# Two queries of a token side by side, and a place of their own for relu and its sum, in a fused time-mix and expert kernel

## The chip, the core and the metric

The kernel runs on one core of a Trainium2 chip. The metric is the device time of one execution in microseconds (us). The core's engines run side by side, each with its own instruction list in a fixed order: TensorE (PE; its weight loads are listed as PEld), VectorE (DVE), ScalarE (ACT), GpSimd (POOL) and SyncE (SP), which issues DMAs. They meet only through semaphores. A matrix product reads two operands from the on-chip memory SBUF: the stationary one, which is loaded into the array as weights first, and the moving one, which is streamed past it. It writes to the accumulator memory PSUM.

## What is computed

The input x has 2 sequences of 2048 tokens with 256 channels, all in float32. After a layer norm two branches are computed and multiplied:

```python
xn = layernorm(x)
s  = timemix(xn)            # RWKV-7 style recurrence, 4 heads of 64 channels
g  = silu(ffn(xn))          # two experts per token, LoRA on a shared 256->1024->256 net
out = x + s * g

# the recurrence of timemix, for each head; S is 64 x 64
sa = S @ a_t                # a_t = -k
S  = S * d_t + outer(sa, b_t) + outer(v_t, kk_t)
y  = S @ r_t

# the experts
inter = xn @ wi.T + bi + (xn @ lora_A[e].T) @ lora_B[e].T
out  += gate_e * (relu(inter) @ wo.T + bo)
```

So each token has two queries, a and r (both are multiplied onto the state), and two keys, b and kk.

## The kernel before

The tokens are handled in 16 blocks of 256 (128 of each sequence). Each block is cut into chunks of 64 tokens (L = 64), so it has 2 chunks (k) for each of 2 sequences (b). Heads come in pairs: `pair` and `par` (which half of the 128 partitions) name a head. Within a chunk the recurrence is turned into matrix products. For this the decays of the state are spread over six levels with h = 1, 2, 4, 8, 16, 32: at level h the chunk is cut in runs of h tokens, and for each pair of neighbouring runs the queries of the second run meet the keys of the first.

The stages of a block are generators: `norm`, `front` (gates of the experts), `mixes` (projections that give r, a, b, kk, v), `levels`, `chunks` (carries the state over, gives y, group norm, output) and `experts`. Each of them yields numbers, the times at which its next step is due, counted in turns; a block begins every 12 turns. A heap runs the steps of all blocks in the order of these numbers. The instructions of every engine are issued in that order and stay in it. The numbers are in the table `AT`, in which a name such as "rank", "op" or "query4" is the place of a step; `PROFILE`, `PROFILE0`, "first" and "last" spread the experts' steps over the turns. Steps with the same number run in the order of the stages, older blocks first.

The steps and buffers that matter here:

- `AR` (L424) holds a block's queries: 128 partitions x 2 queries x 516, all of a and then all of r; r is shifted by one token. `BK` (L426) holds the keys in the same way. ACT writes r into AR from PSUM (L438) and a (L515); POOL reads r for `rk` (L519).
- `products` (L548) multiplies, at each level, the keys of a chunk (stationary) with the queries of the second runs (moving, 64 columns) for all heads, in 64 x 64 corners of the array. Each float32 product is two PE instructions, so there are 64 for each level. They go to two PSUM tiles `lev`, one for each `par`.
- `take_products` (L554) copies what the level's mask allows of `lev` into the pair matrices `D`: two masked copies (COPY_PREDICATED) per level, each of 512 elements per partition. `D` (L240) has 16 rows of DW = 66 words for each `par`: a row for each (chunk, pair, key, query).
- `decay_on` multiplies the queries of the second runs by the decay so far (DVE, L580) and the keys of the first runs (POOL, L583).
- `first_inverse`, `inverse1`, `transposed` and `inverse2` (L607, L623, L617, L630) build the inverse of a triangular matrix in `X` by levels, with `take_inverse` (L634), a masked copy into X, just before `take_products` of the next level.
- `chunks` uses slices of D as weights (L790, L847: `pair_matrix`), and of AR (L809).
- `last_queries` (L563, L566) and `lastr` (L688) handle the last r of a chunk.
- `experts` goes through eight parts f of the hidden layer: `basep` (PE, L938), `base` (ACT, L940), `lop` (PE, L943), `hs` = lop + base for both experts (DVE, L945), relu in place (ACT, L946), and the sum over the two experts into `hT` (POOL, L947). `fop` (L957) multiplies hT by the second weight. `hs` has two buffers.
- `psf` gives PSUM tiles from a pool of four, in turn. Nearly all stages, `lev`, `basep`, `lop`, `miu` and `op` among them, take theirs from it, so that a product can start only when the tile taken four requests before has been read.

Of the kernel before, what the change touches and what calls it, by code (L numbers as in the profile page):

```python
# [34 lines left out]
def timemix_gated_by_lora_experts(ctx: ExitStack, tc: tile.TileContext, a: dict, out: bass.AP):  # L35
# [50 lines left out]
    def load_x(i):  # L86
# [10 lines left out]
        "stats": 5.82, "root_x": 9.97, "inv_x": 10.32, "xn": 10.79, "xTp": 11.66, "dx": 11.66, "xm": 11.84,  # L97
        "lgp": -0.16, "mixp": 0.44, "top": 0.52, "gt": 2.1, "rank": 3, "ex": 3.27, "vsum": 3.94, "mix12": 2.29,
# [4 lines left out]
        "gmean": 6.13, "ysq": 7.26, "gvar": 7.91, "root_y": 9.38, "inv_y": 10.72, "scale": 10.84, "gp": 11.69,  # L103
        "ygp": 12.23, "op": 14.55, "la": -1.34, "first": 0.46, "last": 0.94, "ex0": 0.8, "ex15": 0.9, "ex16": 0.6,
        "ready": 5.51, "const": 4.33, "rv": -0.8, "sa0": 0.2, "up0": 1.2, "uv0": 2.2, "sa1": 3.2, "up1": 4.2,
        "uv1": 5.2,
    }
    PROFILE = [0.88, 1.2, 0.8, 1.66, 0.32, 1.18, 0.01, 0.5, 1.72, 1.5, 1.03, 1.98]
    PROFILE0 = [0.61, 0.53, 1.28, 1.83, 0.05, 0.7, 0.45, 0.41, 1.6, 1.55, 0.66, 3.1]
# [61 lines left out]
    mask = const.tile([P, len(LEVELS), LMAX], U8, name="mask")  # L171
    maskT = const.tile([P, len(LEVELS), LMAX], U8, name="maskT")

    def mask_parts():
        for m, second in ((mask, 0), (maskT, 1)):
            mf = hold.tile([L, len(LEVELS) * LMAX], F32, name=f"mf{second}")
            nc.gpsimd.memset(mf, 1.0)
            for li, h in enumerate(LEVELS):
                n, lo = LMAX // h, second * h
                mv = mf[:, li * LMAX : (li + 1) * LMAX].rearrange("p (n h) -> p n h", h=h)  # L180
                nc.gpsimd.affine_select(out=mv, in_=mv, compare_op=ALU.is_ge, fill=0.0, base=-lo,
                                        pattern=[[-2 * h, n], [0, h]], channel_multiplier=1)
                nc.gpsimd.affine_select(out=mv, in_=mv, compare_op=ALU.is_ge, fill=0.0, base=lo + h - 1,
                                        pattern=[[2 * h, n], [0, h]], channel_multiplier=-1)
                yield
            nc.gpsimd.tensor_copy(m[half(0)], mf.rearrange("p (l c) -> p l c", c=LMAX))

            nc.sync.dma_start(out=m[half(1)], in_=m[half(0)])
# [27 lines left out]


    def order(h):
        return "n h"

    def mask_of(m, li, h, k):
        v = m[:, li, :].rearrange(f"p (n h) -> p {order(h)}", h=h)
        return v.unsqueeze(1).broadcast_to([P, k, *v.shape[1:]])

    def runs(ap, h, which):

        if len(ap.shape) == 2:
            return ap.rearrange("p (n w h) -> p n w h", w=2, h=h)[:, :, which, :].rearrange(f"p n h -> p {order(h)}")
        return ap.rearrange("p m (n w h) -> p m n w h", w=2, h=h)[:, :, :, which, :].rearrange(f"p m n h -> p m {order(h)}")
# [10 lines left out]
    Dbuf = [hold.tile([P, 2, 8 * NK, DW], F32, name=f"D{j}") for j in range(2)]  # L240
# [147 lines left out]
    def mixes(i):  # L388
# [35 lines left out]
        AR = q["AR"] = sb2.tile([P, 2, 516], F32, tag="AR", name=f"AR{i}")  # L424

        BK = q["BK"] = sb2.tile([P, 2, 2 * SUP], F32, tag="BK", name=f"BK{i}")  # L426
        rv = AR[:, 1, 1:513].rearrange("p (c t) -> p c t", c=2)
        av = AR[:, 0, 0:512].rearrange("p (c t) -> p c t", c=2)
# [96 lines left out]
    def levels(i):  # L525
# [17 lines left out]
        def products(li, h):  # L543
            levp = [psf(f"lev{i}_{h}_{par}").rearrange(f"p (m q {order(h)}) -> p m q {order(h)}", m=4 * NK, q=2, h=h)
                    for par in range(2)]
            for key in range(2):
                for k, pair, b, par, rows, c0 in blocks():
                    matmul(levp[par][half(b), (k * 2 + pair) * 2 + key], BK[rows, key, c0 : c0 + L],  # L548
                           runs(AR[rows, :, c0 : c0 + L], h, 1), start=True, stop=True)
            return levp  # L550

        def take_products(li, h, levp):
            for par in range(2):
                nc.vector.copy_predicated(  # L554
                    runs(D[:, par, :, 0:L], h, 1), mask_of(mask, li, h, 8 * NK),
                    levp[par].rearrange("p m q x y -> p (m q) x y"))

        def last_queries():

            lp = [psf(f"last{i}_{par}")[:, 0 : 4 * NK].unsqueeze(2) for par in range(2)]  # L560
            for key in range(2):
                for k, pair, b, par, rows, c0 in blocks():
                    matmul(lp[par][half(b), (k * 2 + pair) * 2 + key, :], BK[rows, key, c0 : c0 + L],  # L563
                           AR[rows, 1, c0 + L : c0 + L + 1], start=True, stop=True)
            for par in range(2):
                nc.vector.tensor_copy(  # L566
                    D[:, par].rearrange("p (m q) v -> p m q v", q=2)[:, :, 1, L : L + 1], lp[par])

        def decay_on(h):

            np_ = SUP // h
            bpv = q["bp"].rearrange("p (n w) -> p n w", w=2)

            def decay(which):
                v = bpv[:, :, which : which + 1].broadcast_to([P, np_, h]).rearrange(f"p n h -> p {order(h)}")
                return v.unsqueeze(1).broadcast_to([P, 2, *v.shape[1:]])

            yield TURNS * i + AT[f"query{h}"]
            qa = runs(AR[:, :, 0 : 2 * SUP], h, 1)
            nc.vector.tensor_tensor(qa, qa, decay(0), ALU.mult)  # L580
            yield TURNS * i + AT[f"key{h}"]
            ka = runs(BK, h, 0)
            nc.gpsimd.tensor_mul(ka, ka, decay(1))  # L583
# [15 lines left out]
        def by_run(t, h):  # L599
            return t.rearrange(f"p m ({order(h)}) -> p m {order(h)}", h=h)  # L600

        def first_inverse():

            nt = ps_inv.tile([P, 2, 512], F32, tag="inv", name=f"n{i}")[:, :, 0 : NK * 2 * LMAX]
            nt = nt.rearrange("p z (m n) -> p z m n", n=LMAX)
            for k, pair, b, par, rows, c0 in blocks():
                matmul(nt[half(b), par, k * 2 + pair, :], AR[rows, 0, c0 : c0 + L],  # L607
                       runs(BK[rows, 0, c0 : c0 + L], 1, 0).squeeze(2), start=True, stop=True)
            for par in range(2):
                xv = X.rearrange("p (m z) (n w) -> p z m n w", z=2, w=2)[:, par, :, :, 0]  # L610
                nc.vector.copy_predicated(xv, maskT[:, 0, :].unsqueeze(1).broadcast_to([P, NK * 2, LMAX]),
                                          nt[:, par])
# [6 lines left out]
        def inverse1(li, h, m1):  # L619

            m1 = by_run(m1, h)
            for e, k, b, m in each():
                matmul(m1[half(b ^ k), m], D[half(b), e % 2, (k * 2 + e // 2) * 4, 0:L],  # L623
                       runs(X[half(b), m, :], h, 0), start=True, stop=True)
# [40 lines left out]
        for li, h in list(enumerate(LEVELS))[1:]:  # L665
# [17 lines left out]
            else:  # L683
                last_queries()
                lastr = AR[:, 1, 1:513].rearrange("p (m t) -> p m t", t=L)[:, :, L - 1 : L]
# [4 lines left out]
    def chunks(i):  # L690
# [14 lines left out]
        def pair_matrix(k, b, par, pair, key, query):  # L705
            return D[half(b), par, ((k * 2 + pair) * 2 + key) * 2 + query, query : query + L]
# [89 lines left out]
        for k in range(NK):  # L796
# [116 lines left out]
    def experts(i):  # L913
# [18 lines left out]
        hT = sb1.tile([P, DFF // P, SUP], F32, tag="hT", name=f"hT{i}")  # L932
        for f in range(DFF // P):
# [9 lines left out]
            matmul(lop, lBT[:, 0, fc], lat, start=True, stop=True)  # L943
            hs = sb2.tile([P, 2, SUP], F32, tag="hs", name=f"hs{i}_{f}")
            nc.vector.tensor_tensor(hs, lop, bs.unsqueeze(1).broadcast_to([P, 2, SUP]), ALU.add)  # L945
            nc.scalar.activation(hs, hs, AF.Relu)  # L946
            nc.gpsimd.tensor_add(hT[:, f, :], hs[:, 0, :], hs[:, 1, :])  # L947
# [49 lines left out]

    parts = [constants()]
# [4 lines left out]
    while queue:  # L1003
        at, n = queue[0]
        after = next(parts[n], None)
# [41 lines left out]
```

## Time and profile before

| | before |
|---|---|
| runs | 1121.29, 1124.88, 1119.23 us |
| median | 1121.29 us |
| profiled execution, its own time | 1120.85 us |
| its span in the profile | 1119.1 us |
| granted TensorE clock, mean | 0.978 |
| masked copies into D, L554 | 192 instructions, 181.4 us of DVE |
| relu, L946 | 128 instructions, 80.6 us of ACT, 142.5 us idle before them |
| sum over experts, L947 | 128 instructions, 93.5 us of POOL, 205.5 us idle before them |
| loads of D's slices in `inverse1`, L623 | 2560 loads, 46.0 us of PEld |

In the page the busy line gives for each engine its busy time, the share of the span and the number of instructions. The chain follows the work that ended last back from the end, and gives the share of each engine in it. A line of the waits reads "who waited, on whom: us in total, times, longest". A line of the timeline reads "start, duration, engine, line, operation, output<-inputs, sizes and number of instructions merged", and in brackets the idle time of the engine before it and who ended it. In the page's groups, a duration behind a comma is the mean of one instruction in ns. Durations of neighbouring instructions of an engine may overlap a little.

### The profile page before, as it was taken

The numbers are of one execution on the slowest core, as the hardware profiler recorded it, in microseconds if no ns is written. First come the engines' busy times: TensorE is split into PE (matmuls) and PEld (weight loads), VectorE is DVE, ScalarE is ACT, GpSimd is POOL, SyncE is SP. The second block draws the span as 40 slices with busy tenths as digits, with TensorE's granted clock in tenths as the row PEclk, the third lists the DMA queues.
The fourth block names the chain that finished last, engine by engine and source line by source line (L and its number), as shares of the span: only waits on it lengthen the run. The fifth ranks groups of instructions, "written<-read, shape, count | busy, mean of one in ns | idle before, by whom it ended". The sixth has DMA issues, their size and how long they took to land.

```text
span 1119.1 us, 51172 instructions
## 1 busy us (share of the span) xinstructions
PE 1056.6 (94%) x23136; PEld 823.2 (74%) x23136; DVE 720.6 (64%) x1613; ACT 573.0 (51%) x1372; POOL 659.6 (59%) x852
## 2 busy tenths in 40 slices
PE   6999999999999998999999999999999999999997
PEld 3677777777777776786777877777777777777865
DVE  5365866666585664757667576766767666685645
ACT  2625546372644636555463645546464553736363
POOL 6373657567474855747466573756757474674541
PEclk8989999999999998999999999999999999999999
DMA  8000000000000000000000000000000000000000
GB/s 230 19 3 2 3 3 4 22 3 22 2 22 3 3 22 3 21 4 3 21 3 22 3 22 3 3 22 4 22 3 13 4 3 13 3 12 3 14 3 20
DMA packets 16073, 17.02 MB, mean 15 GB/s; under 512 B 3248, under 2 KB 15472, under 8 KB 15856
## 3 DMA queue, kind: packets, MB, share of 16 engines
q1 hardware_dynamic: 15696, 13.62, 4.5%
q8 instruction: 182, 2.98, 1.1%
q14 instruction: 35, 0.29, 0.1%
q10 hardware_dynamic: 160, 0.13, 0.0%
HBM read 9.53 MB, written 4.19 MB: 12 GB/s over the span
## 4 chain that ended last, share of the span: by engine, by line
PE 72%; DVE 12%; POOL 4%; issue 3%; ACT 3%; DVEq 0%; POOLq 0%; ACTq 0%
PE fop L957 10%; PE basep L938 8%; PE lev L548 8%; PE lop L943 7%; DVE D L554 5%; PE m1p L623 4%; PE miu L402 3%; PE m1p L617 3%; PE rp L419 3%; PE vp L459 2%; PE op L902 2%; PE kp L468 2%; PE x L630 2%; PE uv L839 2%; PE uv L847 1%
## 5 line engine op out<-in xcount | busy, mean ns | idle before, releaser
L947 POOL TENSOR_TENSOR hT<-hs 128x256 f32<-128x256 f32 x128 | 93.5, 731 | 205.5 <-ACT hs L946 205.5
L554 DVE COPY_PREDICATED D<-mask,lev 128x512 f32<-128x512 uint8 x192 | 181.4, 1022 | 12.7 <-PE lev L548 12.7
L946 ACT ACTIVATE hs<-hs 128x512 f32<-128x512 f32 x128 | 80.6, 629 | 142.5 <-DVE hs L945 125.6
L938 PE MATMUL basep<-xT,w_wiT 128*128 128x256 f32 x512 | 140.7, 399 | 6.8 <-DVE D L554 6.6
L943 PE MATMUL lop<-lat,w_lBT 128*128 128x512 f32 x256 | 138.3, 623 | 4.7 <-ACT lat L931 4.6
L938 PEld LDWEIGHTS basep<-xT,w_wiT 128*128 128x128 f32 x512 | 94.4, 195 | 50.1 <-issue 29.6
L410 POOL TENSOR_TENSOR xd<-xd,xT 128x512 f32<-128x512 f32 x96 | 119.9, 1270 | 19.1 <-DVE xd L408 18.9
L945 DVE TENSOR_TENSOR hs<-lop,base 128x512 f32<-128x512 f32 x128 | 87.4, 683 | 67.4 <-PE lop L943 49.5
L957 PE MATMUL fop<-w_woT,hT 128*128 128x256 f32 x512 | 126.6, 392 | 4.4 <-DVE D L554 3.6
L548 PE MATMUL lev<-AR,BK 64*64 64x64 f32 x6144 | 111.1, 219 | 7.7 <-DVE mx L338 4.6
L548 PEld LDWEIGHTS lev<-AR,BK 64*64 64x64 f32 x6144 | 100.1, 134 | 22.1 <-issue 15.7
L957 PEld LDWEIGHTS fop<-w_woT,hT 128*128 128x128 f32 x512 | 95.5, 193 | 24.7 <-issue 7.9
L583 POOL TENSOR_TENSOR BK<-BK,bp 128x512 f32<-128x512 f32 x80 | 91.2, 1140 | 20.4 <-PE lev L548 20.4
L408 DVE SCALAR_TENSOR_TENSOR xd<-miu,cvec,dx 128x256 f32<-128x256 f32 x192 | 79.4, 475 | 33.9 <-PE miu L402 33.8
L940 ACT ACTIVATE base<-basep,biT 128x256 f32<-128x256 f32 x128 | 60.8, 475 | 26.0 <-PE basep L938 25.8
L623 PEld LDWEIGHTS m1p<-X,D 64*64 64x64 f32 x2560 | 46.0, 136 | 23.3 <-issue 14.2
L634 DVE COPY_PREDICATED X<-maskT,x 128x256 f32<-128x256 uint8 x64 | 32.4, 506 | 47.7 <-PE x L630 47.5
L402 PE MATMUL miu<-mix,w_x_B 32*128 32x256 f32 x384 | 59.0, 411 | 3.8 <-DVE D L554 2.9
L856 ACT COPY Y<-uv 64x128 f32<-64x128 f32 x128 | 33.2, 259 | 53.6 <-DVE ST L852 26.5
L580 DVE TENSOR_TENSOR AR<-AR,bp 128x512 f32<-128x512 f32 x80 | 59.1, 739 | 0.0
L623 PE MATMUL m1p<-X,D 64*64 64x32 f32 x2560 | 53.6, 221 | 3.9 <-DVE D L554 3.2
L943 PEld LDWEIGHTS lop<-lat,w_lBT 128*128 128x128 f32 x256 | 44.2, 192 | 13.6 <-ACT lat L931 6.7
(216 smaller groups left out, 2302.7 us busy)
## 6 DMA issues: line engine op xcount, KB each, us to landing
x<-in_x SPq DMA_DIRECT2D x32, 128.0 KB, 2.8
out<-x SPq DMA_DIRECT2D x30, 128.0 KB, 2.4
w_wiT<-in_wiT SPq DMA_DIRECT2D x1, 1024.0 KB, 8.4
w_woT<-in_woT SPq DMA_DIRECT2D x1, 1024.0 KB, 6.7
w_lBT<-in_lBT SPq DMA_DIRECT2D x1, 512.0 KB, 5.6
w_rWT<-in_rWT SPq DMA_DIRECT2D x1, 256.0 KB, 4.7
w_vWT<-in_vWT SPq DMA_DIRECT2D x1, 256.0 KB, 7.9
w_kWT<-in_kWT SPq DMA_DIRECT2D x1, 256.0 KB, 2.9
```

Source lines behind the costliest of these rows:

```text
L402: matmul(p[:, c, :], xB[r0 : r0 + 32, m, c * P : (c + 1) * P], mix[r0 : r0 + 32, m, :], start=True, stop=True)
L410: nc.gpsimd.tensor_add(xd, xd, xT)
L548: matmul(levp[par][half(b), (k * 2 + pair) * 2 + key], BK[rows, key, c0 : c0 + L], runs(AR[rows, :, c0 : c0 + L], h, 1), start=True, stop= ...
L554: nc.vector.copy_predicated(runs(D[:, par, :, 0:L], h, 1), mask_of(mask, li, h, 8 * NK), levp[par].rearrange("p m q x y -> p (m q) x y"))
L583: nc.gpsimd.tensor_mul(ka, ka, decay(1))
L623: matmul(m1[half(b ^ k), m], D[half(b), e % 2, (k * 2 + e // 2) * 4, 0:L], runs(X[half(b), m, :], h, 0), start=True, stop=True)
L938: matmul(basep, wiT[:, c, fc], xT[:, c, :], start=(c == 0), stop=(c == 1))
L943: matmul(lop, lBT[:, 0, fc], lat, start=True, stop=True)
L945: nc.vector.tensor_tensor(hs, lop, bs.unsqueeze(1).broadcast_to([P, 2, SUP]), ALU.add)
L946: nc.scalar.activation(hs, hs, AF.Relu)
L947: nc.gpsimd.tensor_add(hT[:, f, :], hs[:, 0, :], hs[:, 1, :])
L957: matmul(fop, hT[:, f, k * P : (k + 1) * P], woT[:, f, :], start=(f == 0), stop=(f == DFF // P - 1))
```

## The change

Three things are changed. First, the two queries of a token become neighbours: AR gets the shape 128 x 516 x 2 and D the shape 2 x 8 rows x 66 x 2, with the query as the innermost index; the number of words in D stays the same. At level h, what was two runs of h words with a stride between them becomes one run of 2h words (`query_runs`). The mask of D is widened, so that each token's entry stands twice. All uses follow; a slice of one query, of AR or of D, then takes every second word.

Second, relu and sum of an expert part are taken out of the step of `hs`. They become a step that is put into the heap at 0.05 turn after it, and that is run at the latest before the next but one `hs` or before `fop`.

Third, the numbers in AT and PROFILE0 are others.

```diff
     AT = {
-        "stats": 5.82, "root_x": 9.97, "inv_x": 10.32, "xn": 10.79, "xTp": 11.66, "dx": 11.66, "xm": 11.84,
-        "lgp": -0.16, "mixp": 0.44, "top": 0.52, "gt": 2.1, "rank": 3, "ex": 3.27, "vsum": 3.94, "mix12": 2.29,
-        "mix04": 3.47, "mix35": 4.29, "rp": 4.89, "wkp": 5.23, "vp": 6.6, "kp": 7.84, "ssp": 8.61, "dec": 9.31,
-        "ggp": 9.37, "root_k": 9.8, "kn": 10.55, "av": 11.75, "rk": 11.77, "bop": 13.15, "eye": -0.26, "query1": 0.27,
-        "key1": 0.33, "query2": 1.95, "key2": 2.05, "query4": 3.41, "key4": 3.56, "query8": 5.33, "key8": 5.39,
-        "query16": 7.78, "key16": 7.88, "query32": 9.73, "key32": 9.74, "BT0": -0.24, "BT1": 1.61, "ysum": 5.64,
-        "gmean": 6.13, "ysq": 7.26, "gvar": 7.91, "root_y": 9.38, "inv_y": 10.72, "scale": 10.84, "gp": 11.69,
-        "ygp": 12.23, "op": 14.55, "la": -1.34, "first": 0.46, "last": 0.94, "ex0": 0.8, "ex15": 0.9, "ex16": 0.6,
-        "ready": 5.51, "const": 4.33, "rv": -0.8, "sa0": 0.2, "up0": 1.2, "uv0": 2.2, "sa1": 3.2, "up1": 4.2,
-        "uv1": 5.2,
+        "stats": 5.77, "root_x": 10.18, "inv_x": 10.32, "xn": 10.82, "xTp": 11.66, "dx": 11.66, "xm": 11.84,
+        "lgp": -0.16, "mixp": 0.51, "top": 0.56, "gt": 1.83, "rank": 3, "ex": 3.27, "vsum": 4.02, "mix12": 2.38,
+        "mix04": 3.47, "mix35": 4.35, "rp": 4.87, "wkp": 5.28, "vp": 6.47, "kp": 7.83, "ssp": 8.61, "dec": 9.02,
+        "ggp": 9.37, "root_k": 9.8, "kn": 10.55, "av": 11.69, "rk": 12.04, "bop": 12.52, "eye": -0.33, "query1": 0.38,
+        "key1": 0.54, "query2": 1.94, "key2": 2, "query4": 3.29, "key4": 3.5, "query8": 5.31, "key8": 5.37,
+        "query16": 7.78, "key16": 7.86, "query32": 9.72, "key32": 9.74, "BT0": -0.24, "BT1": 1.65, "ysum": 5.84,
+        "gmean": 6.1, "ysq": 7.11, "gvar": 7.89, "root_y": 9.38, "inv_y": 10.76, "scale": 10.87, "gp": 11.69,
+        "ygp": 12.39, "op": 15, "la": -1.47, "first": 0.46, "last": 0.93, "relu": 0.05, "ex0": 0.8, "ex15": 0.9,
+        "ex16": 0.6, "ready": 5.52, "const": 3.64, "rv": -0.8, "sa0": 0.2, "up0": 1.2, "uv0": 2.2, "sa1": 3.2,
+        "up1": 4.2, "uv1": 5.2,
     }
...
-    PROFILE0 = [0.61, 0.53, 1.28, 1.83, 0.05, 0.7, 0.45, 0.41, 1.6, 1.55, 0.66, 3.1]
+    PROFILE0 = [0.61, 0.53, 1.28, 1.83, 0.03, 0.6, 0.44, 0.43, 1.7, 1.24, 0.96, 2.8]
...
-    mask = const.tile([P, len(LEVELS), LMAX], U8, name="mask")
+    mask = const.tile([P, len(LEVELS), 2 * LMAX], U8, name="mask")
...
+    def query_runs(ap, h):
+
+        if len(ap.shape) == 3:
+            return ap.rearrange("p (n w h) q -> p n w (h q)", w=2, h=h)[:, :, 1, :]
+        return ap.rearrange("p m (n w h) q -> p m n w (h q)", w=2, h=h)[:, :, :, 1, :]
...
-    Dbuf = [hold.tile([P, 2, 8 * NK, DW], F32, name=f"D{j}") for j in range(2)]
+    Dbuf = [hold.tile([P, 2, 4 * NK, DW, 2], F32, name=f"D{j}") for j in range(2)]
...
-        AR = q["AR"] = sb2.tile([P, 2, 516], F32, tag="AR", name=f"AR{i}")
+        AR = q["AR"] = sb2.tile([P, 516, 2], F32, tag="AR", name=f"AR{i}")
...
-        rv = AR[:, 1, 1:513].rearrange("p (c t) -> p c t", c=2)
-        av = AR[:, 0, 0:512].rearrange("p (c t) -> p c t", c=2)
+        rv = AR[:, 1:513, 1].rearrange("p (c t) -> p c t", c=2)
+        av = AR[:, 0:512, 0].rearrange("p (c t) -> p c t", c=2)
...
                     matmul(levp[par][half(b), (k * 2 + pair) * 2 + key], BK[rows, key, c0 : c0 + L],
-                           runs(AR[rows, :, c0 : c0 + L], h, 1), start=True, stop=True)
+                           query_runs(AR[rows, c0 : c0 + L, :], h), start=True, stop=True)
...
-                nc.vector.copy_predicated(
-                    runs(D[:, par, :, 0:L], h, 1), mask_of(mask, li, h, 8 * NK),
-                    levp[par].rearrange("p m q x y -> p (m q) x y"))
+                nc.vector.copy_predicated(query_runs(D[:, par, :, 0:L, :], h), mask_of(mask, li, 2 * h, 4 * NK), levp[par])
...
-            qa = runs(AR[:, :, 0 : 2 * SUP], h, 1)
-            nc.vector.tensor_tensor(qa, qa, decay(0), ALU.mult)
+            qa = query_runs(AR[:, 0 : 2 * SUP, :], h)
+            nc.vector.tensor_tensor(qa, qa, decay(0, 2 * h), ALU.mult)
...
-                matmul(nt[half(b), par, k * 2 + pair, :], AR[rows, 0, c0 : c0 + L],
+                matmul(nt[half(b), par, k * 2 + pair, :], AR[rows, c0 : c0 + L, 0],
...
-                matmul(m1[half(b ^ k), m], D[half(b), e % 2, (k * 2 + e // 2) * 4, 0:L],
+                matmul(m1[half(b ^ k), m], D[half(b), e % 2, (k * 2 + e // 2) * 2, 0:L, 0],
...
-            return D[half(b), par, ((k * 2 + pair) * 2 + key) * 2 + query, query : query + L]
+            return D[half(b), par, (k * 2 + pair) * 2 + key, query : query + L, query]
...
-                            matmul(dst[half(b ^ flip), par, pair, :], AR[half(par), query, c0 : c0 + L],
+                            matmul(dst[half(b ^ flip), par, pair, :], AR[half(par), c0 : c0 + L, query],
...
+            while len(pending) > 1:
+                pending.pop(0)()
             hs = sb2.tile([P, 2, SUP], F32, tag="hs", name=f"hs{i}_{f}")
             nc.vector.tensor_tensor(hs, lop, bs.unsqueeze(1).broadcast_to([P, 2, SUP]), ALU.add)
-            nc.scalar.activation(hs, hs, AF.Relu)
-            nc.gpsimd.tensor_add(hT[:, f, :], hs[:, 0, :], hs[:, 1, :])
+
+            def rest(f=f, hs=hs):
+                nc.scalar.activation(hs, hs, AF.Relu)
+                nc.gpsimd.tensor_add(hT[:, f, :], hs[:, 0, :], hs[:, 1, :])
+
+            pending.append(rest)
+            spawn(later(now[0] + AT["relu"], pending, rest))
...
                 yield next(parts)
+                while pending:
+                    pending.pop(0)()
                 if i == NBLK - 1 and fs:
...
+    def later(at, pending, step):
+        yield at
+        if step in pending:
+            pending.remove(step)
+            step()
+
+    def spawn(part):
+        parts.append(part)
+        heapq.heappush(queue, (next(part), len(parts) - 1))
```

More of the change, by code (lines that the diff above doesn't have):

```diff
@@ L167, in timemix_gated_by_lora_experts @@
                             pattern=[[1, E], [-1, E]], channel_multiplier=0)
-    mask = const.tile([P, len(LEVELS), LMAX], U8, name="mask")
+    mask = const.tile([P, len(LEVELS), 2 * LMAX], U8, name="mask")
     maskT = const.tile([P, len(LEVELS), LMAX], U8, name="maskT")
     def mask_parts():
-        for m, second in ((mask, 0), (maskT, 1)):
-            mf = hold.tile([L, len(LEVELS) * LMAX], F32, name=f"mf{second}")
+        for m, second, w in ((mask, 0, 2), (maskT, 1, 1)):
+            mf = hold.tile([L, len(LEVELS) * LMAX * w], F32, name=f"mf{second}")
             nc.gpsimd.memset(mf, 1.0)
@@ L179, in mask_parts @@
                 n, lo = LMAX // h, second * h
-                mv = mf[:, li * LMAX : (li + 1) * LMAX].rearrange("p (n h) -> p n h", h=h)
+                mv = mf[:, li * LMAX * w : (li + 1) * LMAX * w].rearrange("p (n h) -> p n h", h=h * w)
                 nc.gpsimd.affine_select(out=mv, in_=mv, compare_op=ALU.is_ge, fill=0.0, base=-lo,
-                                        pattern=[[-2 * h, n], [0, h]], channel_multiplier=1)
+                                        pattern=[[-2 * h, n], [0, h * w]], channel_multiplier=1)
                 nc.gpsimd.affine_select(out=mv, in_=mv, compare_op=ALU.is_ge, fill=0.0, base=lo + h - 1,
-                                        pattern=[[2 * h, n], [0, h]], channel_multiplier=-1)
+                                        pattern=[[2 * h, n], [0, h * w]], channel_multiplier=-1)
                 yield
-            nc.gpsimd.tensor_copy(m[half(0)], mf.rearrange("p (l c) -> p l c", c=LMAX))
+            nc.gpsimd.tensor_copy(m[half(0)], mf.rearrange("p (l c) -> p l c", c=LMAX * w))
             nc.sync.dma_start(out=m[half(1)], in_=m[half(0)])
@@ L215, in constants @@
                                       cvec[rows, c, CV["x_time"] : CV["x_time"] + 1])
-    def order(h):
-        return "n h"
     def mask_of(m, li, h, k):
-        v = m[:, li, :].rearrange(f"p (n h) -> p {order(h)}", h=h)
-        return v.unsqueeze(1).broadcast_to([P, k, *v.shape[1:]])
+        return m[:, li, :].rearrange("p (n h) -> p n h", h=h).unsqueeze(1).broadcast_to([P, k, m.shape[2] // h, h])
     def runs(ap, h, which):
         if len(ap.shape) == 2:
-            return ap.rearrange("p (n w h) -> p n w h", w=2, h=h)[:, :, which, :].rearrange(f"p n h -> p {order(h)}")
-        return ap.rearrange("p m (n w h) -> p m n w h", w=2, h=h)[:, :, :, which, :].rearrange(f"p m n h -> p m {order(h)}")
+            return ap.rearrange("p (n w h) -> p n w h", w=2, h=h)[:, :, which, :]
+        return ap.rearrange("p m (n w h) -> p m n w h", w=2, h=h)[:, :, :, which, :]
+    def query_runs(ap, h):
+        if len(ap.shape) == 3:
+            return ap.rearrange("p (n w h) q -> p n w (h q)", w=2, h=h)[:, :, 1, :]
+        return ap.rearrange("p m (n w h) q -> p m n w (h q)", w=2, h=h)[:, :, :, 1, :]
     xtsel = const.tile([P, 2, H], F32, name="xtsel")
@@ L543, in products @@
         def products(li, h):
-            levp = [psf(f"lev{i}_{h}_{par}").rearrange(f"p (m q {order(h)}) -> p m q {order(h)}", m=4 * NK, q=2, h=h)
-                    for par in range(2)]
+            levp = [psf(f"lev{i}_{h}_{par}").rearrange("p (m n j) -> p m n j", m=4 * NK, j=2 * h) for par in range(2)]
             for key in range(2):
@@ L563, in last_queries @@
                     matmul(lp[par][half(b), (k * 2 + pair) * 2 + key, :], BK[rows, key, c0 : c0 + L],
-                           AR[rows, 1, c0 + L : c0 + L + 1], start=True, stop=True)
+                           AR[rows, c0 + L : c0 + L + 1, 1], start=True, stop=True)
             for par in range(2):
-                nc.vector.tensor_copy(
-                    D[:, par].rearrange("p (m q) v -> p m q v", q=2)[:, :, 1, L : L + 1], lp[par])
+                nc.vector.tensor_copy(D[:, par, :, L : L + 1, 1], lp[par])
         def decay_on(h):
@@ L572, in decay_on, with decay @@
             bpv = q["bp"].rearrange("p (n w) -> p n w", w=2)
-            def decay(which):
-                v = bpv[:, :, which : which + 1].broadcast_to([P, np_, h]).rearrange(f"p n h -> p {order(h)}")
-                return v.unsqueeze(1).broadcast_to([P, 2, *v.shape[1:]])
+            def decay(which, n):
+                return bpv[:, :, which : which + 1].broadcast_to([P, np_, n])
             yield TURNS * i + AT[f"query{h}"]
-            qa = runs(AR[:, :, 0 : 2 * SUP], h, 1)
-            nc.vector.tensor_tensor(qa, qa, decay(0), ALU.mult)
+            qa = query_runs(AR[:, 0 : 2 * SUP, :], h)
+            nc.vector.tensor_tensor(qa, qa, decay(0, 2 * h), ALU.mult)
             yield TURNS * i + AT[f"key{h}"]
             ka = runs(BK, h, 0)
-            nc.gpsimd.tensor_mul(ka, ka, decay(1))
+            nc.gpsimd.tensor_mul(ka, ka, decay(1, h).unsqueeze(1).broadcast_to([P, 2, np_, h]))
             nbp = sb2.tile([P, np_], F32, tag=f"bp{2 * h}", name=f"bp{i}_{2 * h}", bufs=3 if h == LMAX else 1)
@@ L599, in by_run @@
         def by_run(t, h):
-            return t.rearrange(f"p m ({order(h)}) -> p m {order(h)}", h=h)
+            return t.rearrange(f"p m (n h) -> p m n h", h=h)
         def first_inverse():
@@ L684, in levels @@
                 last_queries()
-                lastr = AR[:, 1, 1:513].rearrange("p (m t) -> p m t", t=L)[:, :, L - 1 : L]
+                lastr = AR[:, 1:513, 1].rearrange("p (m t) -> p m t", t=L)[:, :, L - 1 : L]
                 zp = ps_inv.tile([P, 2, 512], F32, tag="inv", name=f"z{i}_{h}")[:, :, 0 : NK * 2 * h]
@@ L932, in experts @@
         hT = sb1.tile([P, DFF // P, SUP], F32, tag="hT", name=f"hT{i}")
+        pending = []
         for f in range(DFF // P):
@@ L996, in experts_at @@
             done += cost
+    now = [0]
+    def later(at, pending, step):
[6 more added lines that the diff above has]
+        heapq.heappush(queue, (next(part), len(parts) - 1))
     parts = [constants()]
@@ L1004, in timemix_gated_by_lora_experts @@
         at, n = queue[0]
+        now[0] = at
         after = next(parts[n], None)
```

## The prediction

> **What bounds the kernel now.** I read the page first (busy times, chain), then the waits of TensorE, then the waits of all engines, then the timeline of one block.
>
> ```profile
> PE 1056.6 (94%) x23136; PEld 823.2 (74%) x23136; DVE 720.6 (64%) x1613; ACT 573.0 (51%) x1372; POOL 659.6 (59%) x852
> ...
> PE 72%; DVE 12%; POOL 4%; issue 3%; ACT 3%; DVEq 0%; POOLq 0%; ACTq 0%
> ```
>
> PE is the bound: it idles 1119.1 - 1056.6 = 62.5 us. No other engine is near full, so what they save counts only where PE waits for them. Those waits, longest first:
>
> ```profile
> PE xTp L75 <- ACT xn L286: 9.6, 5, 7.4
> PE basep L938 <- DVE D L554: 6.6, 6, 1.3
> PE lev L548 <- DVE mx L338: 4.6, 10, 1.2
> PE lop L943 <- ACT lat L931: 4.6, 3, 3.3
> ...
> PE fop L957 <- DVE D L554: 3.6, 3, 1.6
> PE m1p L623 <- DVE D L554: 3.2, 5, 1.3
> ...
> PE miu L402 <- DVE D L554: 2.9, 2, 1.7
> ```
>
> With latp (1.3) and aap (0.4), PE waits 18.0 us, 18 times, for the masked copy L554: about once a block. The rest of this answer adds up to some 38 us: 13 for other DVE work, 21 for ACT, 4 for POOL. Of all engines' waits two concern the relu:
>
> ```profile
> POOL hT L947 <- ACT hs L946: 205.5, 86, 7.0
> ACT hs L946 <- DVE hs L945: 125.6, 87, 4.2
> ```
>
> ACT stands 125.6 us before relus whose input isn't ready, and POOL 205.5 us before their sums. DVE's timeline of one block shows the copies of L554 (two each, levels 1, 2, 4, 8, 16, 32) and those into X (L634):
>
> ```profile
> 580.11 2.58 DVE L554 COPY_PREDICATED D<-mask,lev 128x512 f32<-128x512 uint8 x2
> ...
> 584.57 2.47 DVE L554 COPY_PREDICATED D<-mask,lev 128x512 f32<-128x512 uint8 x2 [0.30 <-PE lev L548]
> ...
> 596.27 0.71 DVE L634 COPY_PREDICATED X<-maskT,x 128x256 f32<-128x256 uint8 x1
> 596.78 1.86 DVE L554 COPY_PREDICATED D<-mask,lev 128x512 f32<-128x512 uint8 x2
> ...
> 609.32 0.44 DVE L634 COPY_PREDICATED X<-maskT,x 128x256 f32<-128x256 uint8 x1 [0.52 <-PE x L630]
> 609.66 1.57 DVE L554 COPY_PREDICATED D<-mask,lev 128x512 f32<-128x512 uint8 x2
> ...
> 618.18 1.43 DVE L554 COPY_PREDICATED D<-mask,lev 128x512 f32<-128x512 uint8 x2
> ...
> 629.17 1.39 DVE L554 COPY_PREDICATED D<-mask,lev 128x512 f32<-128x512 uint8 x2
> ```
>
> All twelve move 512 elements; time falls as runs lengthen.
>
> **Copies into D.** What costs is pieces of 16 bytes only half written: X with runs of 2 costs 0.71, with runs of 4 (whole pieces) already 0.44. D's rows are 66 x 4 = 264 bytes apart, so every second row starts 8 bytes off, and long runs too have two half pieces there. A copy has 256 half pieces at levels 1 and 2, then 128, 64, 32, 16. From 16 to 128 the pair grows by 1.86 - 1.39 = 0.47 us: 2.1 ns per half piece; 2.47 at level 2 fits (2.40). Without any, a pair would take 1.39 - 32 x 0.0021 = 1.32. After the change rows are 528 bytes apart (33 pieces), and a run holds 2h words: level 1 has 256 half pieces (2.47), all others none. Sum 2.47 + 5 x 1.32 = 9.07 against 11.30: 2.2 us a block, 36 us of DVE in 16 blocks. That takes D's start to lie on a 16-byte boundary, as X's must; if not, only level 1 gains (0.11 a block). I take the first, since every tile here is a multiple of 16 bytes but a few tiny ones.
>
> [...]
>
> **What PE gets of that.** The typical wait, from the same timeline at level 4 (between these lines stand that level's two copies, shown above):
>
> ```profile
> 594.97 0.62 PE L630 MATMUL x<-M,Z 64*64 64x32 f32 x32
> 595.52 1.13 PE L402 MATMUL miu<-mix,w_x_B 32*128 32x256 f32 x8
> 595.93 0.41 DVE L812 TENSOR_TENSOR rhs<-sa,RV 128x256 f32<-128x256 f32 x1
> ...
> 597.96 1.16 PE L938 MATMUL basep<-xT,w_wiT 128*128 128x256 f32 x4 [1.30 <-DVE D L554]
> ```
>
> DVE is late with a queue of small steps, and PE's next product needs the PSUM buffer that the first copy frees. The first copy shortens by (1.86 - 1.32) / 2 = 0.27 us; what went faster before it is lost in DVE's idle time. 18 x 0.27 = 5 us gained; bounds 0 (misaligned D, or DVE's queue takes it back) and 18. Next late there are rank and its one-hots, which stay in the queue ahead. Level 1's copies, 0.11 shorter, stand before the 10 waits of lev on mx: 1 us.
>
> **Products of a level (lev).** The moving queries now come as one run of 2h instead of two of h. The timeline has 64 instructions in 1.18 us at level 1 (step 2), 1.17 at level 2, 1.11 to 1.16 above; level 1 takes on the pattern of level 2. Nothing either way.
>
> **Strided weights, the price.** Slices of D and AR that are loaded as weights (m1p 2560 loads, sa 1024, uv from D 1024, n 512, rvp 512: 5632) now take every second word. No load in the trace is strided. These products are held by their loads: 64 with one moving column (last) take as long, 1.11 us, as 64 with 64 columns, so 17.3 ns each, 97 us in all; a slower load is paid in full. Nearest rows: moving operands with step 2, in lev at level 1 (1.18 against 1.11) and in n (32 in 0.61 to 0.64 against 0.62 for x). So 0 to 0.07 us per 64, 0 to 6 us (a strided load isn't faster than a dense one); I take 1, as n shows none.
>
> [...]
>
> **Other accesses to AR.** ACT writes it twice a block (587 and 634 ns), DVE decays it (728 ns with step 2, 681 otherwise), POOL reads it for rk (1088). Bounds: 0 to +0.05 us for ACT and DVE, and for rk up to the 1521 against 1140 that POOL's decay L583 takes with step 2, 0.4 a block. POOL idles 11.5 us before that step L583 of level 1, 0.7 a block, which covers it; uncovered, 6 us. I take 0. The mask's twelve selects (about 270 ns of POOL) double in width at the start: at most 3 us beside other work, 0.
>
> **Relu and sum.** No instruction is added. A relu enters ACT's queue 0.05 turn (of 66 / 12 = 5.5 us: 0.3 us) later, so what is listed within that time goes ahead of its wait; behind a waiting relu stand base, M, Z, U and their waiters. DVE waits 14.0 us for base, PE 21 us for ACT in all, but 7.4 of xn's and the 3.3 for lat were no relu's doing. I take a gain of 2; bounds: 6 gained, and 4 lost where the last sums reach fop late (0.8 us now).
>
> **Places.** The planner's new list moves steps by up to 0.7 turn and could remove or add up to a third of the 38 us of other waits: 13 either way. op goes to the place of rank, so that DVE's two gate steps (0.88) come just before rank; hs leaves that spot in exchange. I take a gain of 2, since the old list left DVE queued at the costliest wait.
>
> **Sum.** 5 + 1 + 2 + 2 - 1 = 9 us. The profiled execution took 1120.85 (span 1119.1), 0.4 under the median of 1121.29: 1120.85 - 9 = 1112.
>
> **Rivals.** *Nothing shows (1117 to 1126)*: DVE's gain falls where PE doesn't wait. For it: of the 2.2 us a block, 1.2 come at level 2 (2.47 to 1.32), where PE hardly waits for the copies. Against: the 18 us of waits are there, and nearly all are at level 4. *Slower*: strided weights. One mechanism, in m1p, sa, uv, n and rvp; it decides from 10% a load (9.7 us), which eats the gain; were loads to pay as level 2's copy does (2.47 / 1.39), 0.78 x 97 = 76 us, 1188; at a quarter, 24 us, 1136. Against: moving step 2 is nearly free. *Places go wrong*: 13 us of new waits less 6 of gain, 1128. *All D waits go and the places fit*: 18 + 13 - 1 = 30, 1091. *D is misaligned*: copies keep 11.2 us a block and the gain is some 3 us, 1118.
>
> **Numbers.** Forecast 1112 (faster, 1100 to 1115): 0.45; the large gain, 1091 to 1100: 0.1; nothing shows or misaligned D: 0.22; strided weights: 0.14; wrong places: 0.09. Faster by over 0.5% (about what a measurement of this kernel can tell: its three runs spread by that much) 0.55, within 0.22, slower 0.23. The range 1095 to 1134 leaves out dearer loads and the largest gain. The likeliest case's own range is 1100 to 1118.
>
> **Right or wrong in the new profile.** L554's pairs: 2.5, then 1.3 at five levels, busy near 145 us (181.4 now). The wait after x at level 4 near 1.0 us. 32 loads of m1p within 0.62 to 0.67 us, PE's busy time within 6 us of 1056.6; longer loads would make the prediction wrong, as would new waits of PE on ACT or POOL.

## The result and the profile after

The changed kernel takes 1114.59 us in the median of 15 runs, the kernel before 1118.38 us in 15 runs, the three shown above among them. The ratio is 0.9963, 95% interval 0.9949 to 0.9978: faster by 0.4%, or some 4 us of the 9 in the prediction's sum, and within the 0.5% that it called no change. The profiled execution of the changed kernel took 1112.51 us (span 1110.5).

Busy times and the chain, from the page of the changed kernel:

```profile
PE 1051.7 (95%) x23136; PEld 823.5 (74%) x23136; DVE 692.7 (62%) x1613; ACT 575.6 (52%) x1372; POOL 667.7 (60%) x852
...
PE 76%; DVE 11%; ACT 3%; POOL 2%; issue 2%; ACTq 0%; DVEq 0%; POOLq 0%
```

DVE has lost 28 us of work (720.6 to 692.7), and PE, the bound, still idles 58.8 us (62.5 before). The copies did what was asked of them. DVE's timeline of one block, the six pairs of copies into D:

```profile
578.66 2.53 DVE L556 COPY_PREDICATED D<-mask,lev 128x512 f32<-128x512 uint8 x2
...
583.05 1.31 DVE L556 COPY_PREDICATED D<-mask,lev 128x512 f32<-128x512 uint8 x2 [0.28 <-PE lev L550]
...
595.96 1.32 DVE L556 COPY_PREDICATED D<-mask,lev 128x512 f32<-128x512 uint8 x2
...
606.93 1.33 DVE L556 COPY_PREDICATED D<-mask,lev 128x512 f32<-128x512 uint8 x2
...
615.33 1.32 DVE L556 COPY_PREDICATED D<-mask,lev 128x512 f32<-128x512 uint8 x2
...
626.33 1.33 DVE L556 COPY_PREDICATED D<-mask,lev 128x512 f32<-128x512 uint8 x2
```

Only level 1 still takes 2.5 us. But PE's waits for these copies are nearly as long as before; from the waits of PE:

```profile
PE basep L937 <- DVE D L556: 8.6, 6, 1.6
PE lop L942 <- ACT lat L929: 5.7, 3, 3.3
PE lev L550 <- DVE mx L341: 4.3, 10, 1.2
PE fop L965 <- DVE D L556: 3.2, 3, 1.6
PE miu L405 <- DVE D L556: 2.7, 3, 1.4
...
PE m1p L621 <- DVE D L556: 1.6, 3, 1.3
```

With latp (0.9) and aap (0.2) that is 17.2 us, against 18.0. The single wait at level 4 has grown from 1.30 to 1.63 us. The timeline of all engines ahead of it shows why:

```profile
592.96 0.28 DVE L361 TENSOR_REDUCE rank<-gt 128x16 f32<-128x128 f32 x1
593.20 0.74 POOL L950 TENSOR_TENSOR hT<-hs 128x256 f32<-128x256 f32 x1
593.27 1.93 DVE L364 TENSOR_SCALAR oh<-rank 128x16 f32<-128x16 f32 x2
593.52 0.63 PE L628 MATMUL x<-M,Z 64*64 64x32 f32 x32
593.89 1.27 POOL L906 TENSOR_TENSOR x<-x,gate 128x512 f32<-128x512 f32 x1
594.08 1.13 PE L405 MATMUL miu<-mix,w_x_B 32*128 32x256 f32 x8
595.11 0.41 DVE L810 TENSOR_TENSOR rhs<-sa,RV 128x256 f32<-128x256 f32 x1
595.45 0.70 DVE L632 COPY_PREDICATED X<-maskT,x 128x256 f32<-128x256 uint8 x1
...
595.96 1.32 DVE L556 COPY_PREDICATED D<-mask,lev 128x512 f32<-128x512 uint8 x2
596.84 0.45 PE L937 MATMUL basep<-xT,w_wiT 128*128 128x256 f32 x1 [1.63 <-DVE D L556]
```

The two one-hot comparisons of `rank` (oh) write 16 elements each and take 1.93 us together: 0.70 and 1.31 us. The same comparison takes 0.16 us at its shortest. Here the first one ends 0.03 us after POOL's sum into hT, and the second, at 595.20, 0.04 us after POOL's instruction on x has ended at 595.16. In this profile all 16 such pairs end 0.03 to 0.11 us after a POOL instruction has ended: the comparisons end when POOL's instructions do. Everything that PE waits for stands behind them on DVE. In the kernel before, the same place looks like this:

```profile
594.65 1.37 DVE L361 TENSOR_SCALAR oh<-rank 128x16 f32<-128x16 f32 x2
594.70 1.28 POOL L908 TENSOR_TENSOR x<-x,gate 128x512 f32<-128x512 f32 x1
...
595.93 0.73 POOL L947 TENSOR_TENSOR hT<-hs 128x256 f32<-128x256 f32 x1
```

There one comparison ran free (0.17 us) and only the other waited x out (1.29 us); now a sum stands ahead of x, and each comparison waits one out. In the instructions of oh no wait of DVE for POOL is listed: the time passes inside the comparisons. So, unlike what the opening of this document says, these two engines don't meet through semaphores alone here; the price is up to 1.32 us for one comparison of 16 elements, against 0.16 at the shortest. By what way POOL holds DVE, the trace does not show.

### The profile page after: what moved, and what is told of

Same layout as the page of the kernel before. It is cut to its first block, busy times and chain, and to the rows that moved or that the text cites. A ratio compares the mean times of both kernels' runs of the same rounds, so it can differ in the third digit from the quotient of the medians.

```text
span 1110.5 us, 51157 instructions
## 1 busy us (share of the span) xinstructions
PE 1051.7 (95%) x23136; PEld 823.5 (74%) x23136; DVE 692.7 (62%) x1613; ACT 575.6 (52%) x1372; POOL 667.7 (60%) x852
## 4 chain that ended last, share of the span: by engine, by line
PE 76%; DVE 11%; ACT 3%; POOL 2%; issue 2%; ACTq 0%; DVEq 0%; POOLq 0%
PE fop L965 10%; PE basep L937 9%; PE lop L942 8%; PE lev L550 8%; PE m1p L621 4%; DVE D L556 3%; PE miu L405 3%; PE m1p L615 3%; PE rp L422 3%; PE vp L462 3%; PE kp L471 2%; PE op L900 2%; PE x L628 2%; PE uv L837 2%; DVE oh L364 2%
## 5 line engine op out<-in xcount | busy, mean ns | idle before, releaser
L950 POOL TENSOR_TENSOR hT<-hs 128x256 f32<-128x256 f32 x128 | 93.7, 733 | 184.0 <-ACT hs L949 183.8
L556 DVE COPY_PREDICATED D<-mask,lev 128x512 f32<-128x512 uint8 x192 | 146.6, 823 | 11.5 <-PE lev L550 11.5
L937 PE MATMUL basep<-xT,w_wiT 128*128 128x256 f32 x512 | 138.4, 393 | 8.6 <-DVE D L556 8.6
L949 ACT ACTIVATE hs<-hs 128x512 f32<-128x512 f32 x128 | 80.5, 629 | 107.6 <-DVE hs L946 91.8
L550 PEld LDWEIGHTS lev<-AR,BK 64*64 64x64 f32 x6144 | 101.4, 135 | 21.8 <-issue 13.1
```

The source lines that it names most:

```text
L556: nc.vector.copy_predicated(query_runs(D[:, par, :, 0:L, :], h), mask_of(mask, li, 2 * h, 4 * NK), levp[par])
L937: matmul(basep, wiT[:, c, fc], xT[:, c, :], start=(c == 0), stop=(c == 1))
```

## The experiments

All ratios are against the kernel before, run beside them.

**Layout alone.** AT, PROFILE0 and the relu's step as before:

```diff
 # the changed kernel, with the old numbers in AT and PROFILE0, and in experts():
-            pending.append(rest)
-            spawn(later(now[0] + AT["relu"], pending, rest))
+            nc.scalar.activation(hs, hs, AF.Relu)
+            nc.gpsimd.tensor_add(hT[:, f, :], hs[:, 0, :], hs[:, 1, :])
```

> Layout alone: the queries side by side, with the relu in its old step and all the old places. Theory 1 (the copies' gain reaches PE where DVE queues before the level-4 copies, and the new places gave it back): L554's counterpart at about 147 us of DVE, PE's waits for D fall from 18.0 to about 13, strided weights cost 2 us, so 2 to 4 us faster than before (ratio 0.997). Theory 2 (PE doesn't feel the copies at all): the strided weights alone show, 2 us slower (ratio 1.002).

Ratio 0.9958 (0.9938 to 0.9977). PE's waits for D fell from 18.0 to 15.3 us: basep (6.4), fop (2.9), m1p (2.6), miu (2.2) and two small ones. That is theory 1, with less taken off the waits than the 5 us that it expected; theory 2's slower kernel is excluded. The wait at level 4 of the block shown above is 1.00 us here, with 1.39 us for its two comparisons.

**New places alone.** The kernel before with the new AT and PROFILE0.

> New places alone, on the old layout and the old relu step. Theory 1: slower by 3 to 8 us (ratio 1.003 to 1.007), since the two gate steps, rank and the one-hots now stand in a row before the level-4 copies; PE's waits for D grow from 18.0 to over 22 us. Theory 2 (the places carry what gain there is): 4 us faster (ratio 0.996).

Ratio 1.0192 (1.0162 to 1.0221): 21 us slower, nearly three times the most that theory 1 allowed; theory 2 is out. Waits for D rose to 20.9 us, a little less than theory 1 had, but there is a second loss, in the waits of PE:

```profile
PE basep L938 <- DVE D L554: 8.8, 6, 2.0
PE lev L548 <- POOL BK L583: 6.7, 3, 2.9
```

PE had not waited for POOL's decay of BK at all in the kernel before. The new places put the decay of the keys at level 1 at 0.54 instead of 0.33.

**Layout and relu's place, old places.** The changed kernel with the old AT and PROFILE0 and "relu": 0.05.

> Layout and the relu's own place, with all the old places. Theory 1: as layout alone or up to 2 us better, ratio 0.995 to 0.997; then the new places are worth nothing or less. Theory 2: ratio 1.000 to 1.002.

Ratio 0.9943 (0.9919 to 0.9967), at least as fast as the whole change. The relu's own place adds 0.0015 to the layout's gain, which is within the intervals.

**Rank late.** The changed kernel with two numbers changed:

```diff
-        "rank": 3, "ex": 3.27,
+        "rank": 3.4, "ex": 3.45,
```

> The changed kernel with rank at 3.4 in place of 3 and ex at 3.45 in place of 3.27, so that rank and the one-hots stand behind the level-4 copies on DVE and not before them. Theory 1 (the one-hots, which last till POOL's instruction ends, hold the copies that PE waits for): PE's wait after x at level 4 goes from 1.6 us to under 0.3, its waits for D from 17 to under 8 us, and the time falls by about 9 us to 1105 (ratio to before 0.988). Theory 2 (another wait takes its place): within 2 us of the changed kernel, ratio 0.995 to 0.998.

Ratio 0.9854 (0.9825 to 0.9883), 12 us under the changed kernel. From the timeline, the wait at level 4 and the one-hots, which now come after it:

```profile
588.45 1.32 DVE L556 COPY_PREDICATED D<-mask,lev 128x512 f32<-128x512 uint8 x2
...
589.33 1.10 PE L937 MATMUL basep<-xT,w_wiT 128*128 128x256 f32 x4 [0.43 <-DVE D L556]
...
590.28 0.27 DVE L361 TENSOR_REDUCE rank<-gt 128x16 f32<-128x128 f32 x1
...
590.59 0.25 DVE L364 TENSOR_SCALAR oh<-rank 128x16 f32<-128x16 f32 x2
```

1.63 us have become 0.43, and PE's waits for D 17.2 have become 8.4, both a little above what theory 1 named. That is theory 1 all the same, and more time than it asked for: PE idles 5.7 us less (53.1 against 58.8), and its own busy time is 6.7 us shorter as well (1045.0 against 1051.7), for which no run here shows the cause. New are two waits for BK, 2.3 us in all; the 1.9 us that PE waited once for rank are gone.

**Layout and new places, without the relu's place.**

> The changed kernel with the relu and its sum back in the step of hs (layout and new places only). Theory 1a (the new places fit only a relu of its own place: without it POOL's sums stand before the decay of the keys at level 1, as the 6.7 us of PE's waits for BK in the places-only run say): PE waits for BK again, and the ratio to before is 1.008 to 1.016, far above the changed kernel's 0.996. Theory 1b (the places are bad because of the one-hots before the copies, relu or not): the layout takes its 4 to 5 us off the places-only run, 1.012 to 1.015, and no waits for BK. If the relu's place plays no part, 0.996.

Ratio 1.0131 (1.0106 to 1.0157). Both numbers expected cover it, so the waits decide: PE waits 4.8 us for BK here, which it doesn't in the changed kernel, and 19.5 us for D against 17.2 there. That is theory 1a. The relu's place is worth 19 us under the new places and next to nothing under the old ones. One such wait, from PE's timeline, with what follows it:

```profile
188.00 1.89 PE L955 MATMUL fop<-w_woT,hT 128*128 128x256 f32 x8
189.82 0.46 PE L819 MATMUL up<-rhs,Z 64*64 64x64 f32 x16
192.21 1.16 PE L550 MATMUL lev<-AR,BK 64*64 64x64 f32 x64 [1.93 <-POOL BK L581]
...
194.83 2.95 PE L955 MATMUL fop<-w_woT,hT 128*128 128x256 f32 x8
```

and the same stretch in windows (the column after the engines' busy times is the granted PE clock):

```profile
187.00:193.90 6.90, 4.97 (x126) 4.01 (x124) 3.11 (x7) 4.54 (x9) 3.91 (x5) 0.97 0.01 4
193.90:197.30 3.40, 3.40 (x15) 2.91 (x12) 0.83 (x2) 1.42 (x3) 1.46 (x2) 0.55 0.00 0
197.30:200.70 3.40, 3.40 (x109) 2.62 (x108) 2.40 (x9) 0.59 (x3) 1.91 (x3) 1.00 0.02 5
```

Eight products of fop take 1.89 us before the wait and 2.95 after it, at a granted clock of 0.55. So such a wait can be paid twice. Not each is: in the changed kernel the clock averages 0.74 over the 6.6 us after a wait of 1.61 us that ends at 529.47, and stays at 1.00 over the 7.2 us after the one of 1.63 us that ends at 596.84. Over the profiled execution the clock is 0.971 here and 0.988 in the changed kernel; 1136 x 0.029 - 1110 x 0.012 = 20 us of full-speed clock, of the 26 us between the two spans. These two are the lowest clock of the one kernel and the highest of the other, though. Over all runs the means are 0.978 and 0.984, by the same sum an estimated 7 us of the 19 between the medians; PE's idle time, 11.6 us longer in the profile (70.4 against 58.8), would be the rest. That the waits cause the low clock is read from the order of events, not tested by itself.

**Relu's place and new places, on the old layout.**

> The changed kernel on the old layout (relu's own place and new places only). Theory 1a: ratio to before 0.998 to 1.003, that is the changed kernel plus the layout's 4 to 5 us, since relu's place mends what the places broke. Theory 1b: 1.015 to 1.020, as places alone. PE's waits for D above 20 us under both.

Ratio 1.0051 (1.0032 to 1.0071): a little above 1a's number, far from 1b's. The wait for BK is down to 1.8 us, those for D are 22.4 us (basep 9.8, miu 4.8, fop 3.3, m1p 2.8). Under this order of steps the layout is worth 0.0088, twice what it brought alone.

**One-hots on POOL.** The changed kernel, with all places kept:

```diff
-            nc.vector.tensor_scalar(oh[:, :, s, :], rank, float(s), None, ALU.is_equal)
+            nc.gpsimd.tensor_scalar(oh[:, :, s, :], rank, float(s), None, ALU.is_equal)
```

> The changed kernel with the two one-hot comparisons on POOL instead of DVE, in their old place. Theory 1 in its sharper form (the DVE one-hots can't run beside a POOL instruction, and so last up to 1.3 us each): DVE loses some 22 us of one-hots, the wait after x at level 4 goes under 0.3 us, ratio 0.985 to 0.988 as with rank put late. If only rank's own wait held the copies, the ratio stays at 0.995. What speaks against a full gain: POOL must now wait for rank at this place, with x and the sums queued behind.

Ratio 0.9853 (0.9827 to 0.9878), the same as with rank put late. From the instructions of oh:

```profile
L364 POOL TENSOR_SCALAR oh<-rank x32: 236/256/621, 22.2 to 974.3; 128x16 f32<-128x16 f32 x32
```

Min, median and max are in ns: 256 in the median on POOL, while DVE had 704 in the changed kernel. PE's waits for D are 7.9 us. Rank itself still stands before the copies here, so it was the comparisons that held them.

**Rank late in the kernel before.** "rank": 3.42 and "ex": 3.45, nothing else.

> The kernel before with rank at 3.42 in place of 3 and ex at 3.45 in place of 3.27; nothing else. Theory 1: here too the one-hots (16.7 us) hold the copies; PE's waits for D go from 18 to about 10 us (its copies are longer by 0.27 us each), ratio 0.991 to 0.994. If it takes the new layout to gain: 0.998 to 1.002.

Ratio 0.9932 (0.9912 to 0.9952), as theory 1 had it; the waits for D went from 18.0 to 13.5 us (basep 4.5, m1p 3.4, miu 2.3, fop 2.2), less far than the 10 us that it named. Two numbers in a table gain 0.7%, where the whole change gains 0.4%; the two intervals just overlap.

**Aligned rows.** The kernel before with one number changed:

```diff
-DW = 66
+DW = 68
```

> The kernel before with D's rows 68 words apart instead of 66 (272 bytes, a multiple of 16) and nothing else: queries apart as before, weights dense. Theory 1 (half-written 16-byte pieces cost, and at level 4 and above only the rows' start made them): pairs of copies 2.6, 2.5, then 1.33 at the four upper levels; PE's waits for D fall about as with the layout alone (18 to 14 us), with no price for strided weights, so ratio 0.994 to 0.997. Rival (run length costs, not where rows start): pairs as before, 1.86, 1.57, 1.43, 1.39, ratio 1.000.

Ratio 0.9895 (0.9856 to 0.9934), a larger gain than theory 1 had. The pairs of copies of levels 1, 2, 4 and 8 in DVE's timeline of one block:

```profile
505.45 2.51 DVE L554 COPY_PREDICATED D<-mask,lev 128x512 f32<-128x512 uint8 x2
...
509.84 2.48 DVE L554 COPY_PREDICATED D<-mask,lev 128x512 f32<-128x512 uint8 x2 [0.29 <-PE lev L548]
...
522.05 1.32 DVE L554 COPY_PREDICATED D<-mask,lev 128x512 f32<-128x512 uint8 x2
...
532.97 1.30 DVE L554 COPY_PREDICATED D<-mask,lev 128x512 f32<-128x512 uint8 x2
```

The two upper levels take 1.31 and 1.33. Runs of 4 words and more cost nothing extra once the rows start on 16 bytes; the reading of the copies in the prediction is right, and run length alone is out. The interval lies just below that of the layout alone: one pad of two words gets more than the interleaving, which is better only at level 2, where PE hardly waits. PE's waits for D are 12.7 us, against 15.3 with the layout alone; that is 2.6 of the 7 us between the two, and where the rest comes from is not shown.

**All that helped.** First the changed kernel on the old places with rank at 3.42 and ex at 3.45; then the kernel before with DW = 68 and the same two numbers; then that with the relu's own place as well.

> Layout and relu's own place on the old places, with rank at 3.42 and ex at 3.45. If rank's place is the one fault of the new places, the rest of them is worth nothing: ratio 0.984 to 0.988, as for the changed kernel with rank late (0.985). If the rest of the new places is good: 0.989 to 0.993. If they are bad beyond rank: under 0.983.

Ratio 0.9859 (0.9834 to 0.9885), against 0.9854 on the new places: apart from rank, the new places are worth nothing that these intervals can tell.

> The kernel before with rows of D 68 words apart, rank at 3.42 and ex at 3.45: no interleaving, no place for the relu, old places. Theory 1: rank late on the old kernel gave 0.993; shorter level-4 copies take another 3 to 5 us, ratio 0.988 to 0.991. If the level-2 copies (1.2 us a block, which only the interleaving shortens) count too, it stays 3 us or more above the run with layout, relu and rank late.

Ratio 0.9854 (0.9826 to 0.9881), lower than expected, with no interleaving at all.

> The old layout with rows of D 68 words apart, relu's own place, the old places, rank at 3.42 and ex at 3.45. It differs from the run with layout, relu and rank late on the old places (0.986) only in that the queries are not side by side. If the interleaving is worth its level-2 copies (1.2 us of DVE a block): 0.988 to 0.991, slower than that run. If the strided weights (2 us) and the slower accesses to AR eat that: 0.982 to 0.986, equal or faster.

Ratio 0.9804 (0.9770 to 0.9839): 1098.46 us in the median, the fastest kernel of the study. It differs from the first of the three only by the queries lying apart, in rows padded to 68 words; the intervals just overlap (0.9834 to 0.9839), so that the interleaving costs 0.5% against the pad is likely. That it brings nothing beyond aligned rows is shown twice, here and by aligned rows against the layout alone.

## Right or wrong, step by step

**The number.** The 1112 of the sum and the measured 1114.59 lie close by luck. The sum starts from 1120.85, and over 15 runs the kernel before takes 1118.38; from there 9 us would have been 1109, and 3.8 were gained. The layout's terms (copies 5, level 1 another 1, weights -1) were to gain 5 us, and the layout alone gained 4.7. The 4 us of relu and places did not come: the whole change (0.9963) is no faster than the layout alone (0.9958).

**Copies.** Right: forecast 2.47 at level 1 and 1.32 at the others, measured 2.53 and 1.31 to 1.33; 146.6 us in all for 145 forecast. The five pairs near 1.32 fit a D that starts on 16 bytes, and the pad alone shows the cause. Level 1 now writes two adjacent words at a time, half a piece of 16 bytes, and is the one that still takes 2.53 us.

**What PE gets of that: 5 us.** Right in size for the layout alone, which gains 0.42%, 4.7 us, and at level 4 of the block shown its wait is the 1.00 us that was forecast. But PE's waits for D fell by 2.7 us, not 5: in most blocks by about 0.3, as forecast, while in two they grew (0.73 to 1.55 us, 1.29 to 1.61), where the pair of comparisons had grown to 1.96 and 2.00 us. Where the other 2 us of the gain come from is not shown, so the match is in part luck. Wrong for the whole change: the wait after x was to fall to 1.0 us and rose to 1.63, and all waits for D fell by 0.8. The step that failed is "next late there are rank and its one-hots, which stay in the queue ahead". They did stay, but I took their time from before. With the sums of the experts moved, POOL runs hT and x one behind the other beside them, and they grew from 1.37 to 1.93 us, more than the 0.27 that the copy saved. The row was there in the kernel before; its three durations are the shortest, the median and the longest in ns:

```profile
L361 DVE TENSOR_SCALAR oh<-rank x32: 160/294/1305, 19.2 to 989.9; 128x16 f32<-128x16 f32 x32
```

A mean of 0.52 us for 16 elements, against 0.16 at the shortest, was not asked for its cause.

**Places: 2 us gained, 13 either way.** Wrong in sign and size: alone they cost 1.9%, 21 us. **Relu: 2 us gained, between -4 and 6.** Right under the old places (0.15%, not resolved), wrong under the new ones, where it saves 19 us. The two terms were added, but they belong together: the new places make POOL late with BK unless its sums are moved too. On the new layout and with the relu's own place, the new places cost 0.0020 (0.9963 against 0.9943), inside the intervals. Rank's place, which was left as it was, was worth 1.1% of the time.

**Strided weights: 1 us, 0 to 6.** Inside the bounds. The loads' groups of the changed kernel, busy time and mean ns:

```profile
L621 PEld LDWEIGHTS m1p<-X,D 64*64 64x64 f32 x2560 | 46.7, 136 | 21.7 <-issue 14.2 <-PE basep L937 5.3 <-DVE D L556 0.6
...
L807 PEld LDWEIGHTS sa<-ST,AR 64*64 64x64 f32 x1024 | 18.6, 136 | 10.7 <-issue 7.6 <-ACT BT L724 1.5 <-ACT hs L949 1.0
...
L605 PEld LDWEIGHTS n<-BK,AR 64*64 64x64 f32 x512 | 9.8, 135 | 0.5 <-issue 0.5
```

They were 46.0, 17.9 and 9.2 us; with uv (27.8 to 28.6) and rvp (9.5 to 9.2) that is 2.5 us more of busy time, which is the most that PE can have paid. The mean of one load is 0 to 2 ns longer than before (136, 134 and 134 in these three), in rvp 5 ns shorter, and lev's dense loads grew by 1.3 us (100.1 to 101.4) with no change to them, so the price of the stride is hardly to be told from nothing. The bound at 0, that a strided load isn't faster than a dense one, holds in four of these five groups. The step-2 rows of moving operands were the right neighbours, and the rival of slow loads is out. The other accesses to AR: rk rose from 1089 to 1306 ns within its bounds; ACT's writes from 587 to 651 and 627 to 692, a little above the 0.05 us given.

**Which rival came.** "Nothing shows" in its size (a gain under 0.5%), though not for its reason: most of the 2.7 us that the layout alone takes off the waits for D was given back at the very wait that it should have shortened. The idle times around the relu fell as read from the list, POOL's before the sums from 205.5 to 183.8 us and ACT's before the relus from 125.6 to 91.8, but none of it was time of PE's: under the old places the relu's own place gained nothing that the intervals can tell.

## To carry to other kernels

Before an instruction on the path is made cheaper, ask every small one in the queue ahead of it why it takes what it takes: a 16-element step of 0.16 us that shows 0.5 in the mean is waiting for something, and here moving it out of the way gained 12 us where the rewrite had gained 4. Places, and what was moved between them, are one edit: measure them together and never add their terms. And look for the cheap half of a new layout: two words of padding got all of this one's gain that PE could feel.

## What the runs showed of the hardware

A DVE comparison of 16 elements can last until the POOL instruction beside it ends, in the changed kernel up to 1.32 us instead of 0.16; there each of the 16 pairs ended 0.03 to 0.11 us after a POOL instruction. A masked copy paid an estimated 2.1 ns for each 16-byte piece that it covers only by half (levels 4 and 32 of the kernel before: (1.86 - 1.39) us / 2 copies / 112 pieces) to 2.4 ns (level 1 of the changed kernel: (2.53 - 1.32) us / 2 copies / 256 pieces), so that with rows of 264 bytes even runs of 4 words cost 1.86 us a pair of copies, against 1.32 with rows of 272 bytes. Weights taken from every second word loaded nearly as fast as dense ones (112.9 us of busy time against 110.4 over five groups, at most 2 ns more for one load of about 135). After some PE waits, not after all, the granted clock fell to half: from 50 us on, 6 of the 18 waits of 0.85 us and more in the profile of the changed kernel, and 8 of the 21 in that of the kernel before, were followed within 2.1 us by a stretch at 0.50 that lasted 3.4 to 10.2 us. The mean clock of the profiled executions was 0.989 with rank late in the changed kernel, and 0.971 to 0.979 in the three slower kernels with the new places (0.978 in the kernel before).
